# Fifty products of zeros per attention tile on TensorE

## The chip, the cores and the metric

The kernel runs on one core of a Trainium2 chip. Its time is device microseconds of that core; lower is better. TensorE (PE) multiplies matrices, VectorE (DVE) and ScalarE (ACT) work on elements, GpSimd (POOL) issues the indirect gathers, and SyncE (SP) issues most other transfers. Each engine runs its own list of instructions in order; an instruction that needs another engine's result waits for a semaphore. Results of PE go to PSUM, a memory of several banks; DVE and ACT read them from there.

## The reference

A graph of 12,500 nodes (128 features) and 200,000 edges, sorted by destination, passes through two blocks with residuals. The first is attention over edges with 8 heads of 16 features, and it is the only one that the change touches:

```
h = relu(layernorm(x));  q, k, v = h @ Wq.T, h @ Wk.T, h @ Wv.T
scores = (q[dst] * k[src]).sum(per head) / 4 + edge_attr @ We.T
ex     = exp(scores - segment_max(scores, dst)[dst])
x      = x + segment_sum(v[src] * ex, dst) / segment_sum(ex, dst)
```

The second block is three graph convolutions (gather rows by source, add them up by destination, multiply by weights, normalise), which follow once attention is done.

## The kernel before

A first part computes q, k and v for all nodes and stores them in DRAM. `fast()` then holds the attention loop and the convolutions. All loops are unrolled, and the framework orders every engine's instructions before the program runs and places the semaphores: it takes whatever is ready by its own estimate, so instructions of neighbouring tiles stand mixed on each engine, and a product without inputs from the loop can stand elsewhere than where it was written.

The attention loop (L989 and L1038) runs over 106 tiles of 118 destination nodes. A tile has a window of 2048 edges, 16 per partition. For a tile t:

- POOL gathers k and v of the edges' sources in 16 indirect transfers into `kv` (L1051, recorded under the helper's line L150). `kv` has three buffers, so the gathers of tile t+3 wait until tile t has read its `kv` for the last time, at L1110.
- ACT makes a one-hot matrix `oht` (L1054 and the helper L935). PE multiplies it with the tile's queries in four groups of four products into `qe` (L1061, two buffers), and DVE multiplies each group into `kv` (L1062). DVE sums per head (L1065).
- PE adds the edge bias in four products into `sm` (L1072). DVE adds it (L1074) and scans a running maximum within each partition (L1083, L1085).
- The ends of the partitions go through PE (`ends`, L1090 and L1091), are scanned by DVE across partitions (L1095, L1097), and come back through PE (L1099, L1100). DVE merges them (L1103), scans once more and subtracts (L1106); ACT takes the exponential (L1109), and DVE multiplies it into v (`vals`, L1110).
- DVE compares each edge's local destination with `nums`, the numbers 0 to 117 held in PSUM, and makes a second one-hot matrix `oh` (L1116, two buffers). PE adds up the edges in 16 products into `acc` (L1120), and ACT copies the sum out (L1121).

`go_on` (L984) interleaves steps of a sort that the convolutions need later (L715 to L718). Every four tiles, PE also makes small tables for the scans (L1011, L1032), and an epilogue normalises and stores the nodes (from L1135).

An fp32 product is recorded on PE as two passes, each a weight load and a matmul: the 16 products of a tile at L1061 are 32 matmuls and 32 weight loads in the trace. `nums` is a PSUM tile of [128, 118] fp32 (L911), alone in its bank, and is written once (L912).

Of the kernel before, what the change touches and what calls it, by code (L numbers as in the profile page):

```python
# [8 lines left out]
FP = mybir.dt.float32  # L9
BF = mybir.dt.bfloat16  # L10
# [7 lines left out]
P = 128  # L18
# [16 lines left out]
TN = 118  # L35
# [14 lines left out]
def tile_gnn(ctx: ExitStack, tc: tile.TileContext, x, src, dst, ea, eaT, wqkvT, weT, w1, w2, w3, par, out):  # L50
# [4 lines left out]
    nc = tc.nc  # L55
# [97 lines left out]
    with ExitStack() as s:  # L153
        once = s.enter_context(tc.tile_pool(name="once", bufs=1))
        sr = s.enter_context(tc.tile_pool(name="sr", bufs=3))
        ps = s.enter_context(tc.tile_pool(name="ps", bufs=2, space=PSUM))
        ps1 = s.enter_context(tc.tile_pool(name="ps1", bufs=1, space=PSUM))
# [506 lines left out]
    def fast():  # L664
# [234 lines left out]
        with ExitStack() as s:  # L899
            once = s.enter_context(tc.tile_pool(name="once", bufs=1))  # L900
# [7 lines left out]
            ep = s.enter_context(tc.tile_pool(name="ep", bufs=2))  # L908
            ps2 = s.enter_context(tc.tile_pool(name="ps2", bufs=2, space=PSUM))
            ps1 = s.enter_context(tc.tile_pool(name="ps1", bufs=1, space=PSUM))  # L910
            nums = ps1.tile([P, TN], FP, name="nums")  # L911
            nc.vector.tensor_copy(nums, iota_f[:, :TN])  # L912
            shared = [P, 2 * JJ + 2, H]

            wbd = once.tile([P, 4 * H], FP, name="wbd")
# [68 lines left out]
            def go_on(n):  # L984
                for _ in range(n if steps else 0):
                    next(steps, None)

            loaded = 0
            for t0 in range(0, NTT, NG):  # L989
                n = min(NG, NTT - t0)  # L990
# [47 lines left out]
                for t in range(t0, t0 + n):  # L1038
# [19 lines left out]
                    for j in range(0, JJ, 4):  # L1058
                        qe = ps2.tile([P, 4, D], FP, name="qe")
                        for k in range(4):  # L1060
                            nc.tensor.matmul(qe[:, k, :], ohv[:, :, j + k], qt, start=True, stop=True)  # L1061
                        nc.vector.tensor_tensor(qk[:, j:j + 4, :], qe, qk[:, j:j + 4, :], op=ALU.mult)  # L1062
                    sg = scs[t % NV]
                    sc = sg[:, :, :JJ]
                    nc.vector.tensor_reduce(sc.rearrange("p h j -> p j h"),  # L1065
# [24 lines left out]
                    nc.tensor.matmul(ends[:, 0, :], mg[:, :, JJ - 1], ident, start=True, stop=True)  # L1090
                    nc.tensor.matmul(ends[:, 1, :], mx[:, :, 0], ident, start=True, stop=True)  # L1091
                    go_on(1)
                    th = ths[m]
                    r = run[t % 2]
                    nc.vector.tensor_tensor_scan(r[:, 0, 1:], th[:, 0, :], ends[:, 0, :], -BIG,  # L1095
# [3 lines left out]
                    nc.tensor.matmul(far[:, 0, :], r[:, 0, :P], ident[:H, :H], start=True, stop=True)  # L1099
                    nc.tensor.matmul(far[:, 1, :], r[:, 1, 1:], ident[:H, :H], start=True, stop=True)  # L1100
                    go_on(2 if inner else 1)
                    for k, j in ((0, 0), (1, JJ - 1)):
                        nc.vector.scalar_tensor_tensor(mx[:, :, j], far[:, k, :], con[:, k, m:m + 1], mx[:, :, j],  # L1103
                                                       op0=ALU.add, op1=ALU.max)
# [350 lines left out]
    with tc.If(fits) as branch:  # L1455
        fast()
# [46 lines left out]
```

## Time and profile before

| | us |
|---|---|
| median of 3 runs (6908.93 to 6957.83) | 6929.65 |
| the profiled execution | 6996.49 |
| its span, first to last instruction | 6994.6 |
| stretch of the attention loop in it, about | 160 to 3520 |

| stretch of the profiled execution | length us | PE busy | DVE busy | ACT busy | POOL busy | mean granted PE clock |
|---|---|---|---|---|---|---|
| 160 to 3520 (attention) | 3360 | 1849.55 | 1861.39 | 878.00 | 1670.12 | 0.66 |
| 3520 to 6994 (convolutions) | 3474 | 2535.23 | 1313.23 | 594.35 | 1834.86 | 0.86 |

Times are of one profiled execution. PE's matmuls overlap each other and their ends are modelled, so that PE's busy time is not its work at peak. A line of the groups reads: line, engine, operation, output<-inputs, shapes, count, then busy us, mean ns of one, and the idle time of the engine just before them with what ended it. The granted clock is the share of PE's full clock that the throttle let through; in this trace it is either half or full, in stretches of a few us. "Another core or an unknown queue" and "remote" mean that the profile found no instruction whose end fits the end of the wait; with one core in use it is not another core.

### The profile page before, as it was taken

The page shows a single profiled execution, that of the slowest core. Times are in us where ns is not written, and L with a number is a line of the kernel's source. Part 1 is how long each engine was busy: PE and PEld are TensorE (multiplying, and loading weights), DVE is VectorE, ACT ScalarE, POOL GpSimd, SP SyncE. Part 2 cuts the span into 40 slices and gives each one's busy share as a digit, 9 for nine tenths or more (in the row PEclk, how much of TensorE's full clock was granted, in tenths as well). Part 3 has the DMA queues.
Part 4 walks back from the last instruction along what each step waited for, and adds up shares of the span by engine and source line. Part 5 has one row for each costly group of instructions (what it writes and reads, how often), then busy time and mean ns, then how long its engine had stood idle before and what let it go on. Part 6 is the DMA issues. An engine that isn't in the chain of part 4 may idle for free.

```text
span 6994.6 us, 79497 instructions
## 1 busy us (share of the span) xinstructions
PE 4480.9 (64%) x28140; PEld 4142.4 (59%) x28140; DVE 3297.8 (47%) x6145; ACT 1521.5 (22%) x2637; POOL 3518.1 (50%) x3617
## 2 busy tenths in 40 slices
PE   5455555555555555566557777786777776777776
PEld 2455544544444545555557777776777676767775
DVE  7344445565655666557523333352333334333334
ACT  2222222332222322222211211111111111111110
POOL 1444545455454554556435555525555553555552
PEclk9666666666666666667678888898888888888887
DMA  6434443433333433434377777766777776777776
GB/s 179 108 94 109 107 110 101 102 103 97 94 102 93 105 98 103 104 100 115 76 183 211 200 204 202 206 204 188 197 198 198 193 198 179 200 200 195 194 202 160
DMA packets 617743, 1051.02 MB, mean 150 GB/s; under 512 B 191467, under 2 KB 432043, under 8 KB 617233
## 3 DMA queue, kind: packets, MB, share of 16 engines
q1 hardware_dynamic: 434383, 478.08, 27.5%
q0 software_dynamic: 142608, 348.39, 19.0%
q10 hardware_dynamic: 40348, 219.37, 9.1%
q8 instruction: 228, 3.74, 0.2%
q14 instruction: 176, 1.44, 0.1%
HBM read 773.19 MB, written 272.26 MB: 149 GB/s over the span
## 4 chain that ended last, share of the span: by engine, by line
PE 41%; another core or an unknown queue 19%; DVE 16%; issue 12%; DMA 4%; ACT 2%; POOL 1%; SPq 1%; DVEq 0%; ACTq 0%; POOLq 0%
PE gp L1276 12%; PE zp L1320 10%; PE zp L1322 5%; PE qe L1061 5%; PE acc L1120 5%; DVE sc L1065 2%; DVE vals L1110 2%; DVE A L717 2%; DVE kv L1062 2%; DVE oh L1116 1%; PE sm L1072 1%; DVE A L718 1%; ACT stage L1278 1%; PE bank L1382 1%
## 5 line engine op out<-in xcount | busy, mean ns | idle before, releaser
L150 POOL DMA_INDIRECT rows<-t_d,srcO x1908 | 1834.9, 962 | 1605.8 <-issue 492.5
L150 POOL DMA_INDIRECT kv<-kv_d,srcA x1696 | 1678.9, 990 | 1638.1 <-DVE vals L1110 891.2
L1276 PE MATMUL gp<-hs,go 128*117 128x128 f32 x7056 | 1042.1, 305 | 553.3 <-issue 261.8
L1276 PEld LDWEIGHTS gp<-hs,go 128*117 128x117 f32 x7056 | 953.6, 207 | 613.9 <-issue 391.4
L1061 PE MATMUL qe<-qt,oht 128*128 128x128 f32 x3392 | 855.6, 418 | 581.3 <-DVE kv L1062 408.8
L1061 PEld LDWEIGHTS qe<-qt,oht 128*128 128x128 f32 x3392 | 769.8, 309 | 637.5 <-issue 381.5
L1278 ACT COPY stage<-gp 117x512 f32<-117x512 f32 x1008 | 514.4, 534 | 2442.7 <-PE gp L1276 823.1
L1316 DVE TENSOR_TENSOR oh<-nums,dlS 128x1888 f32<-128x1888 f32 x318 | 674.2, 2120 | 755.7 <-PE zp L1320 313.7
L1320 PE MATMUL zp<-oh,mr 128*128 128x118 f32 x6360 | 904.3, 288 | 182.8 <-issue 141.4
L1320 PEld LDWEIGHTS zp<-oh,mr 128*128 128x128 f32 x6360 | 834.2, 204 | 217.2 <-issue 189.0
L1273 DVE TENSOR_SCALAR go<-gi,iota_q 128x468 f32<-128x468 uint8 x1008 | 441.6, 460 | 931.4 <-remote 359.7
L1120 PE MATMUL acc<-vals,oh 128*118 128x137 f32 x3392 | 559.7, 335 | 175.4 <-ACT vals L1112 102.4
L1120 PEld LDWEIGHTS acc<-vals,oh 128*118 128x118 f32 x3392 | 538.0, 230 | 196.5 <-ACT vals L1112 116.6
L1322 PE MATMUL zp<-oh,rows 128*128 128x118 f32 x3816 | 531.4, 286 | 49.6 <-issue 42.2
L1322 PEld LDWEIGHTS zp<-oh,rows 128*128 128x128 f32 x3816 | 492.4, 202 | 57.8 <-issue 50.1
L1062 DVE TENSOR_TENSOR kv<-qe,kv 128x512 f32<-128x512 f32 x424 | 286.5, 679 | 329.7 <-remote 212.8
L1072 PE MATMUL sm<-wbd,ebx 128*128 128x32 f32 x848 | 211.4, 383 | 190.8 <-issue 71.2
L1072 PEld LDWEIGHTS sm<-wbd,ebx 128*128 128x128 f32 x848 | 211.9, 327 | 186.6 <-issue 124.6
L1116 DVE TENSOR_TENSOR oh<-nums,dlA 128x1888 f32<-128x1888 f32 x106 | 223.9, 2113 | 198.7 <-PE qe L1061 89.3
L1054 ACT ACTIVATE oht<-dw_b,niota 128x2048 f32<-128x2048 bf16 x106 | 212.2, 2002 | 388.9 <-remote 200.0
L1099 PE MATMUL sm<-ident,run 8*128 8x8 f32 x212 | 57.1, 340 | 321.1 <-DVE run L1095 177.6
L1099 PEld LDWEIGHTS sm<-ident,run 8*128 8x128 f32 x212 | 47.2, 275 | 343.8 <-DVE run L1095 187.4
(246 smaller groups left out, 3994.7 us busy)
## 6 DMA issues: line engine op xcount, KB each, us to landing
m<-stage ACTq DMA_DIRECT2D x252, 784.0 KB
mr<-m SPq DMA_DIRECT2D x318, 560.0 KB
dw_b<-dlb_d SPq DMA_DIRECT2D x106, 512.0 KB
gi<-gi_d SPq DMA_DIRECT2D x252, 204.8 KB
rows<-t_d,srcO POOLq DMA_INDIRECT x1908
kv<-kv_d,srcA POOLq DMA_INDIRECT x1696
ebx<-in_edge_attrT_dram SPq DMA_DIRECT2D x106, 256.0 KB
mr<-m SPq DMA_DIRECT2D x318, 75.0 KB
```

The source lines that it names most:

```text
L150: nc.gpsimd.indirect_dma_start(out=o, out_offset=None, in_=table[:, :], in_offset=bass.IndirectOffsetOnAxis(ap=idx, axis=0))
L1061: nc.tensor.matmul(qe[:, k, :], ohv[:, :, j + k], qt, start=True, stop=True)
L1062: nc.vector.tensor_tensor(qk[:, j:j + 4, :], qe, qk[:, j:j + 4, :], op=ALU.mult)
L1072: nc.tensor.matmul(bias[:, 4 * k:4 * k + 4, :].rearrange("p j h -> p (j h)"), eb.rearrange("a (p k) -> a k p", k=4)[:, k, :], wbd, start=T ...
L1116: nc.vector.tensor_tensor(oh, nums.unsqueeze(1).to_broadcast(sh), dlA[:, t, :].unsqueeze(2).to_broadcast(sh), op=ALU.is_equal)
L1120: nc.tensor.matmul(acc, oh[:, j, :], va[:, j, :], start=(j == 0), stop=(j == JJ - 1))
L1273: nc.vector.tensor_scalar(go[:, :n], gv[:, a:a + n], iota_q, None, op0=ALU.is_equal)
L1276: nc.tensor.matmul(gp[:, i, :], go[:, i].rearrange("p t k -> p (t k)"), hs[:, g * SG + a + i, :], start=True, stop=True)
L1278: nc.scalar.copy(stage[:, a:a + n, :], gp[:, :n, :])
L1316: nc.vector.tensor_tensor(oh, nums.unsqueeze(1).to_broadcast(sh), dlS[:, t, :].unsqueeze(2).to_broadcast(sh), op=ALU.is_equal)
L1320: nc.tensor.matmul(zp[:, i, :], mr[:q, j, :], oh[:q, j, :], start=False, stop=False)
L1322: nc.tensor.matmul(zp[:, i, :], rows[:, j, :], oh[:, RC + j, :], start=False, stop=(j == JO - 1))
```

## The change

`nums` becomes the first 118 columns of a tile `nums_` that is declared with 512 fp32 columns, the whole bank. A bf16 tile `zeros` of [128, 256] is cleared once. A helper `busy(n)` issues n products of a 128x128 block of these zeros with the 256 columns of zeros, into columns 128 to 383 of the same bank; nothing reads them. Each tile calls it three times, with 14, 12 and 24.

```diff
-            nums = ps1.tile([P, TN], FP, name="nums")
+            nums_ = ps1.tile([P, 4 * P], FP, name="nums")
+            nums = nums_[:, :TN]
             nc.vector.tensor_copy(nums, iota_f[:, :TN])
+            zeros = once.tile([P, 2 * P], BF, name="zeros")
+            nc.vector.memset(zeros, 0.0)
+
+            def busy(n):
+
+                for _ in range(n):
+                    nc.tensor.matmul(nums_[:, P:3 * P], zeros[:, :P], zeros, start=True, stop=True)
+
...
                         nc.vector.tensor_tensor(qk[:, j:j + 4, :], qe, qk[:, j:j + 4, :], op=ALU.mult)
+                    busy(14)
                     sg = scs[t % NV]
...
                     nc.tensor.matmul(ends[:, 1, :], mx[:, :, 0], ident, start=True, stop=True)
                     go_on(1)
+                    busy(12)
                     th = ths[m]
...
                     nc.tensor.matmul(far[:, 1, :], r[:, 1, 1:], ident[:H, :H], start=True, stop=True)
                     go_on(2 if inner else 1)
+                    busy(24)
                     for k, j in ((0, 0), (1, JJ - 1)):
```

## The prediction

> **What bounds the kernel now.** I read the 40 slices first, then the chain that ended last, then the waits of the attention loop, then single tiles in the timeline.
>
> ```profile
> PEclk9666666666666666667678888898888888888887
> ...
> PE 41%; another core or an unknown queue 19%; DVE 16%; issue 12%; DMA 4%; ACT 2%; POOL 1%; SPq 1%; DVEq 0%; ACTq 0%; POOLq 0%
> ...
> L150 POOL DMA_INDIRECT kv<-kv_d,srcA x1696 | 1678.9, 990 | 1638.1 <-DVE vals L1110 891.2
> ```
>
> The attention loop is the first half. PE is busy for 1849.55 of its 3360 us, at a granted clock of 0.66, so there is room for more products and a clock to win. No engine is full; the loop is a ring. POOL issues a tile's 16 gathers in about 20 us (a start every 1.25 us), and waits 891.2 us in all for L1110, which frees a `kv` buffer. So a tile takes 31 us (3360 us over 106 tiles): 20 us of gathers, and the rest of the way to the next L1110.
>
> What holds L1110 up is in the waits of 160 to 3520 us (total us, times, longest):
>
> ```profile
> DVE mg L1103 <- remote: 252.3, 45, 12.7
> DVE run L1095 <- remote: 233.9, 33, 21.2
> DVE kv L1062 <- remote: 212.8, 27, 24.9
> ```
>
> and, of PE's own waits:
>
> ```profile
> PE qe L1061 <- DVE kv L1062: 408.8, 93, 16.8
> PE sm L1099 <- DVE run L1095: 177.6, 36, 15.2
> ...
> PE ends L1090 <- DVE mg L1085: 105.7, 30, 12.2
> PE acc L1120 <- ACT vals L1112: 102.4, 51, 9.7
> ```
>
> L1103, L1095 and L1062 all wait for PE's semaphore, and 699 us of that (6.6 us a tile) end with no PE instruction. The timeline of one tile shows why. Its gathers run from 2034.8 to 2055.2 us (start us, us, engine, line):
>
> ```profile
> 2046.66 0.59 PE L1100 MATMUL sm<-ident,run 8*128 8x8 f32 x2
> ```
>
> ```profile
> 2056.31 0.36 DVE L1103 SCALAR_TENSOR_TENSOR mg<-sm,con,mg 128x8 f32<-128x8 f32 x2 [8.28 <-remote]
> ```
>
> L1100 ends at 2047.25, but DVE sees it only at 2056.31, 1.1 us after the gathers have ended. In gathers that reach 1865 us PE itself slows down; its matmuls (above) and its weight loads (below) alternate:
>
> ```profile
> 1852.15 5.37 PE L1120 MATMUL acc<-vals,oh 128*118 128x137 f32 x26 [7.59 <-issue]
> 1860.06 0.39 PE L1120 MATMUL acc<-vals,oh 128*118 128x137 f32 x1 [2.53 <-issue]
> 1862.85 0.39 PE L1120 MATMUL acc<-vals,oh 128*118 128x137 f32 x1 [2.40 <-issue]
> ```
>
> ```profile
> 1858.64 0.18 PEld L1120 LDWEIGHTS acc<-vals,oh 128*118 128x118 f32 x1 [1.38 <-issue]
> 1861.45 0.27 PEld L1120 LDWEIGHTS acc<-vals,oh 128*118 128x118 f32 x1 [2.63 <-issue]
> ```
>
> After some fast passes, each single instruction takes 1.4 us, until the gathers end. The weight loads, which signal nothing, are as slow as the matmuls. So while gathers run something behind PE drains slowly, **and it seems to count instructions**. In windows of one tile's gathers where this crawl shows, it begins after 102 to 156 PE instructions, mostly over 140 (counted in the trace).
>
> **The change part by part.** It removes and moves nothing. The clearing of `zeros` and the larger `nums_` happen once (below 1 us). It adds, per tile, 50 weight loads and 50 matmuls. The loop now has 18,056 such instructions in its 3360 us, 170 a tile; it will have 270.
>
> *Price of one.* The trace has no bf16 product. Bounds come from two stretches of L1120 of 3 us each (us, PE busy (matmuls), PEld busy (loads), clock, DMA, GB/s):
>
> ```profile
> 2036.20:2039.20 3.00, 3.00 (x27) 3.00 (x28) 1.00 0.78 236
> 1767.00:1770.00 3.00, 3.00 (x15) 3.00 (x15) 0.50 0.93 282
> ```
>
> A pass of 137 fp32 columns takes 3.00/27 = 0.11 us at full and 0.20 us at half clock. 256 bf16 columns hold fewer bytes per row (512 against 548), so I take that; the other end is by columns, 256/137, 0.21 and 0.37 us. Fifty cost 5.5 us at full clock, 10 at half (ends 5.5 and 18.5). The Trainium skill ("TensorE: Matmul & The Clock Gate", section "Back-to-back issue gap") gives N/2.4 ns warm plus 2.5, and N/1.2 cold; by it 256 columns would cost 109 and 213 ns, an estimate that the lower end agrees with.
>
> *What the clock gives.* The same passes gain 0.09 us each when the clock goes from half to full. 1199 of the 3392 passes of L1120 start at half clock: 108 us at most. The small products of the scans gain some 0.1 us per pass, 4 passes a tile on the ring: 42 us. But the largest group, L1061, gains nothing:
>
> ```profile
> 1573.00:1576.00 3.00, 3.00 (x15) 2.99 (x14) 1.00 0.51 167
> 2030.00:2033.00 3.00, 3.00 (x16) 3.00 (x15) 0.50 0.47 61
> ```
>
> It makes 15 passes in 3 us at full clock and 16 at half. The same page's part "The HAM clock gate" promises nearly twice the rate once PE is kept busy; by it the 1955 passes of L1061 that start at half clock would save 0.09 us each too, an estimate of 176 us; these two rows speak against that. So the clock is worth 0 to -150 us; I take -75, as PE will still fall idle in some gathers.
>
> *What the hundred instructions cost in a window of gathers.* In the tile shown above, L1120, L1072, L1090 and L1091 and then L1099 and L1100 run inside one window, about 112 instructions of which the last signals arrive late. With the tile's share of zeros among them it is 212, and only about 145 fit before the crawl. The other 67 (33 products) run when the window is over, at 0.11 to 0.20 us: 3.7 to 6.7 us before the products behind them reach DVE. I take 5 us for each of 106 tiles: +530 us. Nothing hides it, for L1103 to L1110 and the next gathers hang on it. At the low end the zeros stand where PE waits anyway (the four PE waits above hold 794 us, 7.5 a tile, against the 5.5 needed): 0. At the high end every zero is on the ring at half clock: 106 x 10 = 1060 us (1960 by columns).
>
> *The shared bank.* L1116 reads `nums` from the bank that PE now writes. If the two are kept apart, L1116 waits for the tile's zeros, and the next zeros, with all that PE has queued behind them (L1090, L1099, L1061, L1120), wait for L1116 (2.1 us each). I take 0: L1116 of the tile whose L1110 is at 2059.8 ran at 2001.8, 60 us ahead. Without that cover it is 2.1 us a tile, 224 us. It can't gain, as L1116 reads the same data. The Trainium skill ("PSUM — Partial Sum Buffer", section "PSUM bank collisions raise a hardware error") says to guard PSUM by bank rather than by address, even where the columns differ; by it the sum would lie between +0 and +224 us; no run here shows it yet.
>
> *Sum:* 6996.5 - 75 + 530 + 0 = 7451.5 in the profiled execution's terms. That execution is 66.8 us above the median of the runs, so **7385 us** against 6929.65 (+6.6%). The convolutions stay.
>
> **The rivals.**
>
> *The zeros fall into PE's idle time (faster).* For it: 794 us in which PE waits for DVE or ACT. Then only the clock counts: up to -150 us, 6780; if an eighth of the 699 us of remote waits went as well, 6700. It needs the slow drain to count signals and not instructions, as zeros signal little; the slow weight loads speak against it. The point that decides is whether the crawl still begins after some 145 instructions.
>
> *The loss and the gain cancel (same).* If two thirds of the 33 late products hide, +177 stands against -150: 6930 +- 60.
>
> *The windows freeze (much slower).* In the tile shown DVE still works 13 us into the window before it waits. If the zeros stand ahead of L1090 and L1099, their hundred entries fill the drain at once and the ring makes no headway until the gathers end. Losing 12 us a tile is 1272 us: 8200; half of it 7570. For it: the delay of L1100 by 9 us with only a few instructions queued. Against it: other windows run 100 instructions without any delay.
>
> *The change doesn't do what it says.* As the zeros depend on nothing in the loop, the framework may put all 50 in one place. If a product of the ring stands behind them, that is 5.5 to 10 us a tile, 583 to 1060 us: 7510 to 7990, and the clock keeps falling to half between the bursts.
>
> **How the numbers follow.** Forecast 0.42 (7100 to 7650), frozen windows 0.20 (7570 to 8200), one burst on the ring 0.10 (7510 to 7990), cancelled 0.10 (6870 to 6990), faster 0.18 (6700 to 6860). The range of 6790 to 8000 leaves out about half of the frozen windows and half of the faster case. Slower by over 1%: 0.72; within 1%, which is about what the measurement can tell: 0.10; faster: 0.18.
>
> **What would show it.** Right: a granted clock well above 0.66 in the first half, 5300 added matmuls at 0.11 to 0.20 us each, waits "remote" of L1103, L1095 and L1062 well above 699 us, and crawling PE instructions in most windows. The price of a zero and the bank's wait can be read from the new line and from L1116's idle time. The prediction is wrong if the remote waits do not grow although the instructions do, since then the drain does not count instructions; or if L1061 becomes faster at full clock.

## The result, and the profile after

The changed kernel takes 7213.09 us (median of 4 runs, 7185.3 to 7240.95) against 6919.29 us for the kernel before on the same chip (4 runs): a ratio of 1.041, with a 95 % interval of 1.037 to 1.044. It is slower: 283 us above the 6929.65 us that the prediction started from, where +455 was forecast.

In the profiled executions the span grows from 6994.6 to 7239.2 us. The attention loop (until the last sum of its last tile) ends at 3783.7 us instead of 3512.7, 271 us later; the convolutions behind it take 26 us less, which I did not follow up. The lines of the changed kernel's page that answer to those shown of before:

```profile
PEclk9677777777777777788877998988888888888887
...
PE 55%; issue 16%; another core or an unknown queue 14%; DVE 9%; DMA 3%; ACT 2%; POOL 1%; SPq 1%; ACTq 0%; DVEq 0%; POOLq 0%
...
L150 POOL DMA_INDIRECT kv<-kv_d,srcA x1696 | 1678.4, 990 | 1906.2 <-DVE vals L1122 1084.3
L920 PE MATMUL nums<-zeros 128*128 128x256 bf16 x5300 | 880.0, 324 | 258.8 <-issue 218.5
L1070 PE MATMUL qe<-qt,oht 128*128 128x128 f32 x3392 | 852.3, 398 | 209.1 <-issue 153.8
L1132 PE MATMUL acc<-vals,oh 128*118 128x137 f32 x3392 | 487.8, 306 | 178.5 <-ACT vals L1124 99.0
```

(Line numbers have moved: L1061 is now L1070, L1062 is L1071, L1095 is L1106, L1099 is L1110, L1103 is L1115, L1110 is L1122, L1116 is L1128, L1120 is L1132; the zeros are L920.) The clock of the first half is up, from 0.65 to 0.77 between 400 and 2400 us. PE's share of the chain that ended last has grown from 41 to 55 %. The gathers are as long as before (990 ns each), but POOL waits 1084.3 us for the line that frees a `kv`, 193 us more. Between tiles 10 and 90 the time from one L1122 to the next is 34.38 us, before 31.20.

DVE's and PE's waits of 160 to 3800 us (total us, times, longest):

```profile
DVE run L1106 <- remote: 400.9, 36, 19.0
...
DVE mg L1115 <- remote: 121.8, 12, 20.9
...
DVE kv L1071 <- remote: 77.3, 9, 29.5
```

Before, one line of PE's reads:

```profile
PE qe L1061 <- issue: 153.8, 53, 16.0
```

and after:

```profile
PE sm L1110 <- DVE run L1106: 236.2, 25, 15.8
PE nums L920 <- issue: 218.5, 202, 3.1
PE qe L1070 <- issue: 153.8, 163, 2.4
```

The three "remote" waits that I had blamed, 699 us before, are now 600: one has grown, two have shrunk. In the last two lines PE waits for nothing that the profile shows, 365 times for 1 us on average. For the products of L1070 that is the same total as before in three times as many waits; the waits of the zeros are new. One burst of zeros shows them (timeline of PE):

```profile
2209.25 1.65 PE L920 MATMUL nums<-zeros 128*128 128x256 bf16 x12
2211.33 0.27 PE L920 MATMUL nums<-zeros 128*128 128x256 bf16 x1 [0.44 <-issue]
2212.75 0.27 PE L920 MATMUL nums<-zeros 128*128 128x256 bf16 x1 [1.15 <-issue]
2214.14 0.27 PE L920 MATMUL nums<-zeros 128*128 128x256 bf16 x1 [1.12 <-issue]
2214.88 0.58 PE L920 MATMUL nums<-zeros 128*128 128x256 bf16 x2 [0.47 <-issue]
2216.23 4.21 PE L920 MATMUL nums<-zeros 128*128 128x256 bf16 x19 [0.78 <-issue]
```

Thirty-six products stand in a row, twelve run at speed, then some take 0.7 to 1.4 us each: 11 us in all. At full clock the same 36 need 3.9 us. This is the crawl of the prediction, now with zeros in it. I counted it in both traces: PE instructions of the attention loop that start 0.55 to 1.7 us behind the one before them without a recorded wait. Before there are 230, which hold 209 us; now there are 585, which hold 539 us, and 280 of them are zeros. Windows of one tile's gathers in which it shows have grown from 25 to 63 of the 106. But it doesn't belong to the gathers alone: 167 of the 230 and 390 of the 585 fall into such windows, 73 and 67 %, and the windows cover 64 and 60 % of the loop.

Undisturbed, a product of zeros costs what the lower end of my bounds said. Two stretches of L920 (us, PE busy (matmuls), PEld busy (loads), clock, DMA, GB/s):

```profile
2204.60:2207.60 3.00, 3.00 (x14) 1.87 (x13) 0.50 0.36 112
2139.50:2142.50 3.00, 3.00 (x28) 2.70 (x29) 1.00 0.00 0
```

14 products in 3 us at half clock and 28 at full are 0.214 and 0.107 us each (those under way at the edges are counted); the median from start to start is 109 ns at full and 213 ns at half clock.

### The profile page after: what moved, and what is told of

Same layout as the page of the kernel before. It is cut to its first block, busy times and chain, and to the rows that moved or that the text cites. A ratio compares the mean times of both kernels' runs of the same rounds, so it can differ in the third digit from the quotient of the medians.

```text
span 7239.2 us, 90093 instructions
## 1 busy us (share of the span) xinstructions
PE 5159.2 (71%) x33440; PEld 4618.7 (64%) x33440; DVE 3310.4 (46%) x6146; ACT 1512.2 (21%) x2637; POOL 3514.2 (49%) x3617
## 3 DMA queue, kind: packets, MB, share of 16 engines
q14 instruction: 176, 1.44, 0.1%
## 4 chain that ended last, share of the span: by engine, by line
PE 55%; issue 16%; another core or an unknown queue 14%; DVE 9%; DMA 3%; ACT 2%; POOL 1%; SPq 1%; ACTq 0%; DVEq 0%; POOLq 0%
PE gp L1288 11%; PE zp L1332 10%; PE nums L920 9%; PE qe L1070 7%; PE zp L1334 6%; PE acc L1132 4%; PE sm L1082 2%; DVE sc L1075 1%; DVE oh L1128 1%; PE zp L1207 1%; POOL rows L150 1%; PE bank L1394 1%; DVE vals L1122 1%; PE bank L1415 1%
## 5 line engine op out<-in xcount | busy, mean ns | idle before, releaser
L150 POOL DMA_INDIRECT kv<-kv_d,srcA x1696 | 1678.4, 990 | 1906.2 <-DVE vals L1122 1084.3
L920 PE MATMUL nums<-zeros 128*128 128x256 bf16 x5300 | 880.0, 324 | 258.8 <-issue 218.5
L1070 PE MATMUL qe<-qt,oht 128*128 128x128 f32 x3392 | 852.3, 398 | 209.1 <-issue 153.8
L1332 PE MATMUL zp<-oh,mr 128*128 128x118 f32 x6360 | 875.9, 284 | 156.3 <-issue 126.4
L1070 PEld LDWEIGHTS qe<-qt,oht 128*128 128x128 f32 x3392 | 780.6, 309 | 261.5 <-issue 195.1
L1332 PEld LDWEIGHTS zp<-oh,mr 128*128 128x128 f32 x6360 | 817.5, 201 | 179.3 <-issue 162.6
L920 PEld LDWEIGHTS <-zeros 128*128 128x128 bf16 x5300 | 610.3, 119 | 456.5 <-issue 314.7
L1132 PE MATMUL acc<-vals,oh 128*118 128x137 f32 x3392 | 487.8, 306 | 178.5 <-ACT vals L1124 99.0
L1132 PEld LDWEIGHTS acc<-vals,oh 128*118 128x118 f32 x3392 | 467.1, 204 | 196.0 <-ACT vals L1124 106.4
L1071 DVE TENSOR_TENSOR kv<-qe,kv 128x512 f32<-128x512 f32 x424 | 287.7, 683 | 386.9 <-PE qe L1070 268.6
L1110 PE MATMUL sm<-ident,run 8*128 8x8 f32 x212 | 50.2, 307 | 362.1 <-DVE run L1106 236.2
L1110 PEld LDWEIGHTS sm<-ident,run 8*128 8x128 f32 x212 | 40.4, 236 | 387.2 <-DVE run L1106 246.6
L1122 DVE TENSOR_TENSOR vals<-kv,sm 128x2048 f32<-128x2048 f32 x106 | 241.8, 2281 | 67.6 <-ACT sm L1121 67.1
```

What stands on the lines that cost most here:

```text
L150: nc.gpsimd.indirect_dma_start(out=o, out_offset=None, in_=table[:, :], in_offset=bass.IndirectOffsetOnAxis(ap=idx, axis=0))
L920: nc.tensor.matmul(nums_[:, P:3 * P], zeros[:, :P], zeros, start=True, stop=True)
L1122: nc.vector.tensor_tensor(vh[:, :, :, :C], kv[:, :, D:].rearrange("p j (h c) -> p j h c", h=H), ex.unsqueeze(3).to_broadcast([P, JJ, H, C] ...
L1132: nc.tensor.matmul(acc, oh[:, j, :], va[:, j, :], start=(j == 0), stop=(j == JJ - 1))
L1332: nc.tensor.matmul(zp[:, i, :], mr[:q, j, :], oh[:q, j, :], start=False, stop=False)
```

## The experiments

Two theories were to be told apart, and a third one beside them. **A:** PE's instructions drain slowly while gathers run, and what counts is their number (the theory of the prediction). **B:** what counts is the PE time of the zeros, which delays the products of the tile queued behind them. **C:** PE's zeros and DVE's reads of `nums` are kept apart because they share a bank.

All experiments ran on two chips on which the kernel before takes 5127 to 5160 us, not 6920 as where the result was measured; I take that for another chip, though nothing recorded says whether it was one or only in another condition. So the experiments tell what the zeros cost on these two; what is particular to the chip of the result has only the two traces above. Each ratio is against the kernel before in the same set of runs, with its 95 % interval.

**The two kernels themselves, on the other chips.** The kernel before, once more:

> The kernel before, for its trace on the chip on which it takes some 5130 us. Theory A needs a crawl here too if the drain belongs to the gathers: PE instructions 0.7 to 1.4 us apart in a quarter of the windows. Theory B: no crawl, a period of some 21 us per tile set by the gathers (POOL idle under 0.5 us between a tile's gathers and the next ones'), and PE idle for 4 to 6 us of each, which is the room that the zeros fill first.

The changed kernel, once more:

> The changed kernel once more, as the standard of this set: 50 products of 256 columns of zeros per tile. Theory A (while gathers run, PE's signals come late by the number of its instructions, so the 100 instructions are what costs): +3.7 to +4.4 % on a chip on which the kernel before takes some 6900 us and its trace shows the crawl; within 1 % on one on which it takes some 5130 us, where no window crawled. Theory B (the PE time of the zeros, 50 x 0.11 = 5.5 us per tile, delays the products behind them): wherever the tile's period is the gathers' (21 us), about as in wide33, +2 to +3 %; the same +2 to +4 % on the slower chip. Theory C (PE and DVE are kept apart on the shared bank): at most 60 us, +0.8 to +1.2 %, on either.

Before: 5139.06 us in one run, with 21.0 us per tile and 4.6 us of idle PE in each, as B had it. The change: 5307.7 us against 5160.2, a ratio of 1.0286 (1.0269 to 1.0303), +147 us. No crawl is in either trace: not one PE instruction of the attention loop starts 0.55 to 1.7 us late without a recorded wait. Theory A's "within 1 % where nothing crawls" is refuted, so the crawl is not needed for a loss. Page of the kernel before on this chip:

```profile
PEclk9777777776777777777799999999999989999997
...
PE 33%; DMA 29%; POOL 16%; DVE 11%; issue 8%; ACT 2%; SPq 1%; DVEq 0%; POOLq 0%; ACTq 0%; another core or an unknown queue 0%
...
L150 POOL DMA_INDIRECT kv<-kv_d,srcA x1696 | 1721.1, 1015 | 541.2 <-issue 477.3
```

and of the changed kernel:

```profile
PEclk9889999898889989988889999989999989999997
...
PE 56%; DMA 23%; DVE 7%; POOL 7%; issue 4%; ACT 2%; SPq 1%; ACTq 0%; DVEq 0%; POOLq 0%; another core or an unknown queue 0%
...
L150 POOL DMA_INDIRECT kv<-kv_d,srcA x1696 | 1706.9, 1006 | 739.1 <-issue 467.3
L920 PE MATMUL nums<-zeros 128*128 128x256 bf16 x5300 | 723.5, 293 | 26.1 <-DVE oh L1128 21.7
```

Here a tile takes 21.0 us before, and POOL stands still for only 0.30 us between a tile's gathers and the next ones': attention is as fast as the gathers are issued. With the zeros a tile takes 23.3 us, and POOL waits 2.46 us. The stretch of 400 to 2400 us in both (length, then busy PE, PEld, DVE, ACT, POOL, clock, DMA share, GB/s), before:

```profile
400.00:2400.00 2000.00, 1560.73 (x7965) 1445.57 (x7965) 1682.45 (x3289) 781.04 (x1146) 1527.96 (x1494) 0.73 0.57 148
```

and after:

```profile
400.00:2400.00 2000.00, 1876.52 (x11642) 1707.36 (x11641) 1552.24 (x3046) 718.51 (x1080) 1374.95 (x1372) 0.91 0.55 137
```

PE was busy 78 % of the time and is busy 94 % of it. POOL, busy 76 % before, gives way (69 %). What POOL now waits for is L1122, which frees a `kv` (waits of POOL in the same stretch):

```profile
POOL kv L150 <- DVE vals L1122: 178.0, 24, 18.0
```

The 24 waits belong to some 86 tiles; in the others POOL still goes straight on. So the loop, which the gathers bound before, is now held up in part of its tiles by the way to L1122, on which PE is the engine that is nearly full.

**As many instructions, a sixteenth of the columns** (run twice):

```diff
-                    nc.tensor.matmul(nums_[:, P:3 * P], zeros[:, :P], zeros, start=True, stop=True)
+                    nc.tensor.matmul(nums_[:, P:P + 16], zeros[:, :P], zeros[:, :16], start=True, stop=True)
```

> The 50 products per tile keep their weight loads and their places, but have 16 columns instead of 256. Theory A (while a tile's gathers run, PE is held back by the number of its instructions): still slower than before, by 200 to 370 us, and the granted clock of the attention stretch stays near 0.66 to 0.70. Theory B (the zeros cost by the time that they take on PE): at most 150 us slower, since a product shrinks from 0.11 us to about its weight load. Theory C (the zeros cost by the wait between PE and L1128 on the shared bank): as the change, 230 to 360 us slower, and with nothing else changed.

> The 50 products of zeros per tile have 16 columns each instead of 256: as many PE instructions and the same shared bank, but a sixth or so of the PE time and hardly any rise of the clock. Theory A: on a chip whose trace crawls it costs as much as the changed kernel or more (+4 to +6 %, since the clock gives nothing back); where nothing crawls, under 1 %. Theory B: under 1 % on either chip. Theory C: the same as the changed kernel's, +0.8 to +1.2 %, on either.

5161.99 us against 5130.48 (1.0062, 1.0043 to 1.0081) and 5185.08 against 5160.2 (1.0049, 1.0032 to 1.0066). The count of instructions and the shared bank are the change's, and a fifth of its loss is left. That speaks for B and, as the bank is shared here too, against C as the cause of the whole; the fifth that is left could be the bank's.

**As many columns, a different number of instructions.** A third fewer:

```diff
-                    nc.tensor.matmul(nums_[:, P:3 * P], zeros[:, :P], zeros, start=True, stop=True)
+                    nc.tensor.matmul(nums_[:, P:4 * P].rearrange('p (a b) -> p a b', b=P), zeros[:, :P],
+                                     zeros[:, :P].unsqueeze(1).to_broadcast([P, 3, P]), start=True, stop=True)
...
-                    busy(14)
+                    busy(9)
...
-                    busy(12)
+                    busy(8)
...
-                    busy(24)
+                    busy(16)
```

> 33 products of 384 columns per tile (9, 8 and 16) instead of 50 of 256: nearly the same columns (12672 against 12800), a third fewer PE instructions. Theory A: the gross cost of some 370 us (294 measured plus some 75 that the clock gives back) falls by a third, so 130 to 220 us slower than before. Theory B: unchanged, 250 to 340 us slower. Theory C: unchanged or a little more, as each product still writes the bank.

and twice as many:

```diff
-                    nc.tensor.matmul(nums_[:, P:3 * P], zeros[:, :P], zeros, start=True, stop=True)
+                    nc.tensor.matmul(nums_[:, P:2 * P], zeros[:, :P], zeros[:, :P], start=True, stop=True)
...
-                    busy(14)
+                    busy(28)
...
-                    busy(12)
+                    busy(24)
...
-                    busy(24)
+                    busy(48)
```

> 100 products of zeros per tile of 128 columns each, in place of 50 of 256: as many columns in all, twice the instructions. Theory B (PE's time): 128 columns should take 0.055 to 0.06 us at full clock, half of the 0.109 of 256 columns, so 5.5 to 6 us of PE per tile as before and the changed kernel's loss, +2.5 to +3.3 % where the kernel before takes 5130 us. Theory A (the count of PE instructions): where nothing crawls, as narrow16, under 1.5 %; on a chip that crawls, 200 more instructions per tile instead of 100, about twice the changed kernel's +4.1 %, +7 to +10 %. Theory C: twice as many writes into the shared bank, but no longer groups: as the changed kernel.

33 products of 384 columns: 5263.3 us, 1.0267 (1.0249 to 1.0285). 100 products of 128 columns: 5281.92 us against 5127.24, 1.029 (1.0267 to 1.0313). The change's 50 of 256: 1.0286. Three times as many instructions in the one as in the other, and losses within 0.3 % of each other: this is the clearest of the experiments. The 133 us of the 33 products lie in A's stated range and below B's, but both ranges were set from the loss on the chip of the result; against the change's 147 us here, A's third less would be 98. Where nothing crawls, the loss goes with the columns, which are PE time, and not with the count.

**Less and more of it.** Only the 24 behind the merge:

```diff
-                    busy(14)
+                    busy(0)
...
-                    busy(12)
+                    busy(0)
```

> Only the 24 products of zeros behind the merge of the scans are left (the 14 and the 12 are taken out): 24 x 0.11 = 2.6 us of PE and 48 instructions per tile. Theory A: on a chip that crawls, where about 145 instructions fit before it, 48 more than 170 per tile: half to a quarter of the changed kernel's loss. Theory B: about half of the changed kernel's loss (24 of 50), on either chip. Theory C: the bank's wait needs one group of zeros only, so it stays at nearly the whole of its share, up to 60 us.

and 100 per tile (28, 24 and 48 in the three places):

```diff
-                    busy(14)
+                    busy(28)
...
-                    busy(12)
+                    busy(24)
...
-                    busy(24)
+                    busy(48)
```

> 100 products of zeros per tile (28, 24 and 48): 11 us of PE and 200 instructions per tile more than before. Theory A: on a chip that crawls, 100 more instructions at the 2.3 to 3.2 us per hundred that the changed kernel lost: another 250 to 400 us, ratio 1.08 to 1.11; where nothing crawls, no more than twice the changed kernel's loss. Theory B: the loss grows faster than the count, since PE's work per tile (about 17 us of its own and 11 of zeros) exceeds the 21 us of a period of gathers: +10 to +20 % where a period is 21 us, +6 to +9 % where it is 31. Theory C: the bank's wait is per group and grows by the longer groups only, about twice the changed kernel's.

24 products: 5218.79 us, 1.0116 (1.0099 to 1.0133), +59 us. 50: +147 us. 100: 5678.47 us, 1.1009 (1.0991 to 1.1028), +518 us. B had said so: half the zeros cost a little less than half, twice the zeros cost 3.5 times as much, at the lower end of the 10 to 20 % expected. C had said that the bank costs at most 60 us and that twice the zeros cost about twice as much. The 59 us of the 24 products alone would fit it, the 147 and the 518 don't. PE does wait before its zeros for L1128, the reader of the bank: 56.7 us in all with 16 columns (second run), 43.8 with the 24 products, 42.9 with 100 of 128 columns, 21.7 with the change and 4.7 with 100 of 256 (where L1128 in turn waits 43.4 us for zeros). The kernel with the longest of these waits loses only 25 us, so that over half of them cost nothing there.

PE's time per tile shows why the price rises. The time of a tile is that between tiles 10 and 90; PE's busy time is its share of 400 to 2400 us, times the time of a tile, and the zeros' part is L920's in the same stretch:

| us per tile | a tile | PE busy | of it zeros | PE idle |
|---|---|---|---|---|
| before, other chips | 21.00 | 16.39 | - | 4.61 |
| 50 of 16 columns (second run) | 21.42 | 17.84 | 1.63 | 3.59 |
| 24 of 256 | 21.77 | 19.01 | 3.70 | 2.76 |
| 33 of 384 | 22.66 | 21.23 | 6.56 | 1.43 |
| 50 of 256 (the change) | 23.30 | 21.86 | 6.81 | 1.44 |
| 100 of 128 | 22.71 | 21.64 | 7.02 | 1.06 |
| 100 of 256 | 26.54 | 26.10 | 11.96 | 0.44 |
| before, chip of the result | 31.20 | 16.85 | - | 14.35 |
| the change, chip of the result | 34.38 | 23.88 | 8.50 | 10.49 |

With the change the zeros take 6.81 us; PE's own work falls by 1.33 us (to 15.05; the clock has risen), 3.17 us of idle time take up a part of the rest, and 2.3 us are left, by which the tile is longer. That is book-keeping, as busy and idle time add up to the tile; what it shows is how the price rises. The first 3.70 us of zeros (24 products) lengthen a tile by 0.77 us, a fifth of their time; the next 3.11 (50) by 1.53, half of it; the next 5.15 (100) by 3.24, five eighths. The less idle time is left, the more of a zero's own time is paid for.

**Without indirect gathers.** The control, which has no zeros and loads 16 x 128 consecutive rows in place of those that the edges name (so it leaves out the real gather):

```diff
+                    r0 = (t % 80) * TN
...
-                        gather(kv[:, j, :], kv_d, srcA[:, t, j:j + 1])
+                        nc.sync.dma_start(kv[:, j, :], kv_d[r0 + j * P:r0 + (j + 1) * P, :])
```

> Control for the next one, without products of zeros: the rows of kv come by 16 plain transfers of consecutive rows from SP in place of 16 indirect gathers from POOL (which leaves out the real gather, so that other rows are worked on; all later work is the same in amount). Theory A: where windows crawl, the crawl and the late signals go with the gathers, and attention ends several hundred us earlier. Theory B: on the chip with 21 us per tile the period falls from the gathers' 21 us to that of the next engine, DVE or PE, 17 to 19 us, some 200 to 400 us less in all, a ratio of 0.92 to 0.96.

and the same edit in the changed kernel:

> The kernel without indirect gathers (plain transfers of consecutive rows, as in the control) with the 50 products of zeros per tile. Theory A (the loss needs gathers in flight): within 1 % of the control. Theory B (PE's time): without the gathers' period nothing covers the zeros; PE's 15 to 16 us of its own and 5.5 to 6.8 us of zeros make 21 to 23 us per tile against 17 to 19 in the control: +3 to +5 us per tile, +300 to +500 us, 6 to 10 % above the control, more than the 147 us that the change costs with the gathers. Theory C: at most 60 us.

The control takes 5201.33 us (1.0129, 1.0112 to 1.0146), not the 0.92 to 0.96 that was expected: a tile takes 21.68 us although POOL does nothing in the loop. So the gathers were not the only thing that held a tile at 21 us; the way through PE, DVE and ACT seems nearly as long (in the chain that ended last, PE's L1062 and L1121 hold 35 % of 400 to 2400 us; no run varies that way alone). With the zeros it takes 5399.94 us, +199 us or 3.8 % on the control, and a tile takes 23.93 us. Theory A (within 1 % without gathers) is refuted again; B has the direction, but its +300 to +500 us were too many, because its control was not as fast as assumed. PE's idle time goes from 5.07 to 2.15 us.

**Zeros in a bank of their own.** DVE reads the numbers 0 to 117 from SBUF instead of PSUM, which frees their bank. Without zeros:

```diff
-            nums_ = ps1.tile([P, 4 * P], FP, name="nums")
-            nums = nums_[:, :TN]
-            nc.vector.tensor_copy(nums, iota_f[:, :TN])
+            nums = iota_f[:, :TN]
```

> The kernel before with nums read from SBUF (iota_f) instead of PSUM, no zeros: the control for the next run. All theories: within 100 us of before; L1116 may change its duration of 2.12 us.

and with the 50 products of zeros in the bank that nobody reads (the first line of that diff stays):

> The change with nums read from SBUF, so that the zeros have their bank to themselves and neither engine waits for the other over it. Theory A and B: slower than the control without zeros by 200 to 380 us. Theory C: at most 100 us slower than the control.

5289.58 us (1.0317, 1.03 to 1.0334) and 5384.41 us (1.0503, 1.0479 to 1.0526). The control itself was a surprise. Its page:

```profile
L150 POOL DMA_INDIRECT kv<-kv_d,srcA x1696 | 1883.6, 1111 | 535.6 <-issue 487.5
```

A gather takes 1111 ns instead of 1015, and a tile 22.50 us instead of 21.00. On that control the zeros cost 95 us (1.8 %), less than the change's 147. Of what was expected only C's "at most 100 us" holds; A's and B's 200 to 380 is missed. That is no proof for C: the longer gathers leave PE more idle time to fill (5.66 us a tile against 4.61), and a tile takes 23.60 us, no less than the 23.30 of the change, in which the bank is shared. But the difference of the two losses, 52 us or a third of the change's, may be the bank's; these two runs can't tell the bank from the longer gathers. So C is at most a part of the loss.

## Why the prediction was right or wrong

The direction was right and the size too large: 7213 us against 7385, +4.1 % against +6.6 %. The direction is in part luck, since the term that made the forecast slower, +530 us, is the one whose mechanism the runs don't bear out. By its own steps:

*Price of a product: right.* 0.11 us at full clock was taken and 0.109 measured; 0.20 at half, and 0.213. The other end, by columns of fp32, is out. The rule of the Trainium skill ("TensorE: Matmul & The Clock Gate", section "Back-to-back issue gap") gave 109 and 213 ns, and the measured medians are these to the nanosecond. The section calls its rule that of an isolated product and gives 81 ns for 128 columns in a stream of weight loads and products; the zeros here are such a stream and took 56 ns for 128 columns, so the isolated rule held for them too.

*The clock: half right.* It rose from 0.65 to 0.77, and PE's own work per tile fell from 16.85 to 15.38 us on the chip of the result. Times 106 that is 156 us, at the far end of my 0 to 150, though not all of it lies on the way that sets the end, and I can't tell how much does. The claim about the groups holds: L1132 (before L1120) fell from 559.7 to 487.8 us, while L1070 (before L1061) stayed at 852.3 against 855.6. From start to start, L1061's passes take 219 ns at half and at full clock in both traces of before; L1120's take 228 and 116 ns.

*The hundred instructions in a window of gathers, +530 us: this is the step that failed.* It said that 33 products of every tile come 5 us late because the drain counts instructions, and that nothing hides it. The prediction named its own test, the "remote" waits of L1103, L1095 and L1062, which should grow well above 699 us. They are 600.

The late signals themselves are real. Each of the 105 waits before ended within 0.04 us of a recorded update of PE's semaphore, and that update stands 1.5 to 16.1 us (median 5.8) behind the recorded end of the last product that signals; in the same kernel's trace on another chip no update of the loop comes more than 0.03 us behind. (Ends of products are modelled, so that this can be a late signal or a product that ended late.) But with 5300 more products they hardly became more: 559 updates of the loop before and 585 after lie over 1.5 us behind. As zeros signal too, some of the late waits may now be put down to a zero; counted without that, the time for which the three lines waited although the products that they read had ended fell from 812 to 655 us.

The other sign that it named, the crawl, did spread: from 25 to 63 of the 106 windows. It begins in them after 139 PE instructions before and 150 after (medians where three or more crawl; the middle halves are 60 to 146 and 117 to 178), which a count of instructions would give. So a limit on the number isn't refuted on that chip; what is refuted is that it shows as late signals at 5 us a tile, and that it is needed for a loss.

What the runs put in its place has two parts. The first is shown: PE time. On chips without any crawl the zeros cost 2.9 %, they cost it by columns and not by instructions, and 3.2 of their 6.8 us per tile are covered by PE's idle time.

The second belongs to the chip of the result and is only read from its traces: there the zeros take longer. From start to start within their bursts they need 962 us on that chip and 611 us on the other, in the same order on PE; the crawl holds 330 us more of PE's time than before. That is as large as the 271 us by which attention grew, but PE has 10.5 us of idle time per tile left there, so the sum of its busy time doesn't set the tile. The zeros do stand on the chain that ended last, with 17.5 % of 160 to 3784 us, some 635 us. The tiles, split by the crawl, say something too. Between tiles 10 and 90, from one tile's first gather to the next one's, the 63 tiles without crawl took 28.5 us before, and the 17 with it (three instructions or more) 42.3; after, 30 took 31.2 and 41 took 38.2. A tile without crawl is 2.7 us longer, about as on the other chips, and more tiles have the crawl; whether it is the crawl that makes a tile long, two traces don't show.

No experiment ran on that chip: whether narrow zeros would crawl there as much as wide ones, that is, whether theory A holds where there is a crawl, stays open, as does what the crawl is and how the 283 us divide between the two parts.

*The shared bank, 0 taken of 0 to 224 us: about right.* In the trace after, PE waits 31.7 us in all before its zeros for DVE's reader, L1128, and L1128 waits 21.7 us for zeros. DVE's merge L1115 waits 59.1 us for zeros, which is not the bank, as it doesn't read it: PE works in order. On the other chips up to 52 us may be the bank's, as said.

*The rivals.* "The zeros fall into PE's idle time" is true of a part of them: on the other chips idle time takes up 1.85 of their 3.70 us per tile with 24 products, and 3.17 of 6.81 with 50. It failed as a forecast since the part that idle time didn't take was larger than what the clock gave back (3.64 against 1.33 us per tile with the change). "The change doesn't do what it says" was partly right in its premise: 62 % of the zeros stand in PE's order in bursts of 28 and more (36, 28, 45 and 33 are the commonest of these) instead of 14, 12 and 24. Its price of 583 us and more was not. The windows did not freeze: the "remote" waits of the merge, L1103, fell from 252.3 to 121.8 us.

*The profiled execution and the median.* The sum was made in terms of the profiled execution and lowered by 66.8 us; the profiled execution after is 27.9 us above its median. That accounts for 39 us of the difference between the growth of the medians and that of the spans.

## What to carry to other kernels

Work that is "free" because an engine has idle time is free only in part, even while idle time is left, where the round goes through that engine: price it by its own duration per round, and compare that with the engine's idle time per round in the windows, after the gain of the clock. Before a theory that counts instructions is believed, vary the count at equal work and the work at equal count; here two runs of that kind settled it for the chips that they ran on. And a mechanism read from one trace should be looked for in a second one of the same kernel: the late signals and the crawl were real in the trace of before, and on two other chips there were none.

## What the runs showed of the hardware

The same program ran 35 % apart on the chip of the result and on the two others: 6919 against 5130 us, with 31.2 against 21.0 us for a tile, and 198 against 255 GB/s in the convolutions. The single gathers are equally long (990 and 1015 ns), and so are L1061's passes (219 ns). On the slower one PE's instructions sometimes come 0.7 or 1.4 us apart without a recorded cause; on the others never in these loops. Its trace also lacks records: of the transfers' landings 32,040 are there, against 97,179 for the same kernel elsewhere, of PE's semaphore updates 9692 of 10,661. The runs don't tell why, nor whether the two belong together.

A bf16 product takes, start to start at full clock, 25 ns for 16 columns, 56 for 128, 109 for 256 and 163 for 384, each with a weight load of its own; at half clock 27, 107, 213 and 320. In the kernel with 100 products of 128 columns a stretch inside a burst shows it (columns as above), 65 in 3.5 us, those under way at its edges counted:

```profile
547.70:551.20 3.50, 3.50 (x65) 3.50 (x65) 1.00 0.88 221
```

Reading a small operand of DVE from SBUF instead of PSUM made POOL's gathers 10 % longer (1111 against 1015 ns) and the kernel 3.2 % slower, more than 50 products of zeros per tile do. The edit gives L1116 two inputs in SBUF in place of one. The Trainium skill ("GPSIMD Engine Reference", section "Specifications") names contention of GpSimd with just such DVE instructions; the traces agree with it: the 143 gathers that run beside the comparison for over 0.3 us take 2190 ns on average, against 991 ns for 210 such gathers in the kernel before, while those that don't touch it take 1012 against 1018 ns.
